# A relational graph layer on one core: 32 counted nodes in place of 16, and another order of the two edge fronts

## The chip, the cores and the metric

The kernel runs on one core of one Trainium2 chip, as a single launch. The metric is device time in microseconds (us). Before the change it is 2970.67 us, the median of three runs (2969.94 to 2975.62). Engines are TensorE (PE; PEld is its weight load), VectorE (DVE), ScalarE (ACT), GpSimd (POOL) and SyncE (SP).

## What is computed

6250 nodes with 256 features, 100000 edges sorted by target node, 8 edge types. Three relational layers, then a small attention, each followed by a residual and a layer norm:

```
for l in range(3):
    xr  = einsum('nd,rde->rne', h, W_rel[l])
    agg = segment_sum(xr[edge_type, src], dst)        # 100000 edges
    h   = relu(agg + h @ W_root[l] + bias[l])
x = layernorm(x + h)
alpha = softmax(leaky_relu(alpha_l[src] + alpha_r[dst]))   # only the first 6250 edges are used
x = layernorm(x + broadcast(sum_h alpha * xt[dst]))
```

The target of an edge is drawn as 6250 u², u uniform, so the lowest nodes have by far the most edges: the first tiles of 128 edges belong to a handful of nodes each.

## The kernel before

**Tiles.** Edges lie in 782 tiles of 128 (one per SBUF partition), nodes in 49 tiles of 128. The kernel does not multiply each edge by a weight. It first sums the *inputs* of the edges by (target, type), and then multiplies the sums by the eight weights.

**One group of the edge loop** (`layer`, the loop `for i in range(NG + 5)`) is up to GT = 4 edge tiles. `gather` (L499) has GpSimd issue one indirect DMA per tile, which fetches 128 source rows of 1 KB into a buffer `msg`. `onehot` (L483, VectorE) makes a 0/1 matrix of the tile's edges against (type, node in window), R·W wide; W, the number of nodes a tile may span, is 3 to 26. `windows` (L516, TensorE) multiplies the rows by it: two matmuls per tile, which the profile shows as two records each, so four records per tile. `add` (L528, VectorE) adds the result, out of PSUM, into a ring of node tiles S, at a place read from `pos`.

**Two fronts.** The edge tiles are walked from two starting points, both downwards: front 0 (the upper, tiles TM = 410 to 781, wide windows, ring of four node tiles) and front 1 (the lower, tiles 36 to 409, narrow windows, ring of three). `Plan.order` mixes the groups of the two: before, one of each in turn, and six groups of the lower front at the end.

**Dense work.** When the last edge tile of a node tile is added, `dense` (L582, L586) multiplies it by W_root and by the eight W_rel: 36 f32 records of 256 columns. It is a generator; every group takes PIECE = 6 steps of it. `finish` (L606, L609 or L613 to L622) adds the bias and stores the tile, `clear` (L595, ScalarE) zeroes its place in the ring. In the third layer `logits` (L636) and `prepare` (L726 to L762) make what the attention needs.

**Hot nodes.** The first HOT = 16 nodes have so many edges that tiles 0 to 35 are left out of the edge loop (TH = 36). For them `count` (L649 to L666), once, in the first layer, counts how often each source row occurs per (node, type): for a pair of node and edge tile VectorE makes a 0/1 matrix `sel` of 392 columns and TensorE adds it up in PSUM; 138 pairs, two per group from group COUNT_AT = 56. `products` (L692), in each layer, multiplies the counts A (f32) with all rows of the node table: 49 matmuls in 13 loads of up to four node tiles, one load and one product in turn per group from group HOT_AT = 130. Its loads are issued by SyncE and take their buffers from the same pool `mp` (eight buffers of four tiles, in turn) as the gathers.

**What orders the work.** Each engine runs its instructions in program order (`manual_schedule`); between engines there are semaphores. Within a group the program has, in this order: steps of `prepare`, `count` and `products`; the gather; `onehot` of the group four ahead; `logits`; `finish` and `clear` of what `dense` ended; the windows; up to six dense steps; the adds; the transposes of the next node tile (`turn`, L560, L563); `fold` (L569, L571). GpSimd may run ahead of TensorE as far as free buffers in `mp` let it.

```
msg = gather(i)
vals = places(i)
...
wins = windows(i, msg, ohs.pop(0))
...
add(i, wins, vals)
```

Of the kernel before, what the change touches and what calls it, by code (L numbers as in the profile page):

```python
# [10 lines left out]
F32 = mybir.dt.float32  # L11
I32 = mybir.dt.int32
BF16 = mybir.dt.bfloat16
AF = mybir.ActivationFunctionType
ALU = mybir.AluOpType
AX = mybir.AxisListType
# [4 lines left out]
P = 128  # L21
EPS = 1e-5
GT = 4
NS = (4, 3)
PAD = 32
MARGIN = 800
HOT = 16
SELS = 6
LOWS = 17
COUNT_AT = 56  # L30
HOT_AT = 130
NEAR = 450
DB = 32
PREP_AT = 164
PIECE = 6
WB = 32
AHEAD = 4
LEAD = 6
GWIN = 256
# [4 lines left out]
class Plan:  # L44
# [35 lines left out]
    def order(self):  # L80

        g = [list(range(k, min(k + GT, self.T))) for k in range(self.TH, self.T, GT)][::-1]
        a = [[t for t in k if t >= self.TM] for k in g if k[-1] >= self.TM]
        b = [[t for t in k if t < self.TM] for k in g if k[0] < self.TM]
        n = max(1, len(b) - LEAD)
        seq, k = [], 0
        for i, g in enumerate(b):
            while k < len(a) and k * n <= i * len(a):
                seq.append((0, a[k]))
                k += 1  # L90
            seq.append((1, g))
        return seq + [(0, g) for g in a[k:]]

# [25 lines left out]
def kernel(  # L119
# [14 lines left out]
    nc = tc.nc  # L134
    N, D = x.shape
    E = src.shape[0]
    L, R = w_rel.shape[0], w_rel.shape[1]
    H, DH = attn_l.shape
    KC = D // P
    pl = Plan(N, E, R)  # L140
    NT, T, CH, WMAX = pl.NT, pl.T, pl.CH, pl.WMAX
# [7 lines left out]
    flag = const.tile([1, 1], I32, name="flag")  # L149
# [3 lines left out]

    bad = nc.values_load(flag[0:1, 0:1], min_val=0, max_val=6 * T)
    with tc.If(bad > 0):
# [3 lines left out]
def fast(tc, const, pl, x, xs, src, dst, edge_type, w_rel, w_root, bias, weight,  # L159
         attn_l, attn_r, out, flag):  # L160
    nc = tc.nc
# [8 lines left out]
    with ExitStack() as top:  # L170
# [16 lines left out]

        A = tab.tile([P, NT, HOT * R], F32, name="A")

# [12 lines left out]
        with ExitStack() as s:  # L202
# [4 lines left out]
            xp = s.enter_context(tc.tile_pool(name="xp", bufs=3))  # L207
            hp = s.enter_context(tc.tile_pool(name="hp", bufs=1))
            ps_w = s.enter_context(tc.tile_pool(name="ps_w", bufs=4, space=PSUM))
# [32 lines left out]
            with tc.manual_schedule():  # L242
                for l in range(L):
                    wr, wo = load_w(l)
                    opn = layer(
                        tc, pl, l, l == L - 1, groups, ready, S, hold, A, hk, hl, idx, key, pos,
                        iota, ident, wr, wo, bias_b, x, xs, eps, w1x, altab, y,
                        (al3, ga, hif, yT0, lane, dst, iota_p),
                        mp, op, xp, hp, ps_w, ps_d, ps_t, H)

# [211 lines left out]

def layer(tc, pl, l, final, groups, ready, S, hold, A, hk, hl, idx, key, pos, iota, ident, wr, wo,
          bias_b, x, xs, eps, w1x, altab, y, att, mp, op, xp, hp, ps_w, ps_d, ps_t, H):
    nc = tc.nc
# [107 lines left out]
    def cols(f, j):  # L573
        at = (j % NS[f]) * P
        return S[f][:, :, at:at + P]
# [64 lines left out]
    def count():  # L640

        lows, made, pc = {}, [], None
        pairs = [(n, t) for n in range(HOT) for t in pl.hot_tiles(n)]
        for m in range(len(pairs) + SELS - 2):
# [13 lines left out]
            if m >= SELS - 2:  # L658
                n, t, oh = made.pop(0)
                tiles = pl.hot_tiles(n)  # L660
                if t == tiles[0]:
                    pc = ps_d.tile([P, 512], F32, name="pd")
                nc.tensor.matmul(pc[:, :NT * R], lows[t], oh, start=(t == tiles[0]),  # L663
                                 stop=(t == tiles[-1]))
                if t == tiles[-1]:
                    nc.scalar.copy(A[:, :, n * R:(n + 1) * R],  # L666
                                   pc[:, :NT * R].rearrange("p (j r) -> p j r", r=R))
            yield

    def products():  # L670
# [14 lines left out]

        sums = hp.tile([P, D], F32, name="sums")
        for js in loads:
            t = load(js)
            yield
            ph = ps_d.tile([P, 512], F32, name="pd")  # L690
            for n, j in enumerate(js):
                nc.tensor.matmul(ph[:, :D], A[:, j], t[:, n], start=(n == 0), stop=(j == js[-1]))  # L692
            yield
            if js[0] == 0:
                nc.vector.tensor_copy(sums, ph[:, :D])
            else:
                nc.vector.tensor_tensor(sums, sums, ph[:, :D], ALU.add)
        pt = ps_t.tile([P, 4 * P], F32, name="pt")
        for k in range(KC):
            nc.tensor.transpose(pt[:, k * P:(k + 1) * P], sums[:, k * P:(k + 1) * P], ident)  # L700
        for k in range(KC):
            o = cols(1, 0)[:, k * R:(k + 1) * R, :HOT]
            nc.vector.tensor_tensor(
                o, o, pt[:, k * P:k * P + HOT * R].rearrange("p (n r) -> p r n", r=R), ALU.add)
        yield
# [79 lines left out]
    for i in range(NG + 5):  # L785
# [4 lines left out]
        for _ in range(2 if i >= COUNT_AT else 0):  # L790
            next(counting, None)
        if i >= HOT_AT:
            next(hot, None)
# [81 lines left out]
def halves(A):  # L875

    v = A.rearrange("p j s -> p (j s)").bitcast(BF16)
    n = v.shape[1] // 2
    return v[:, :n], v[:, n:]
# [498 lines left out]
```

## Time and profile before

| what | value |
|---|---|
| median of the runs shown | 2970.67 us |
| the profiled execution: its time, its span | 2981.72 us, 2980.0 us |
| mean granted TensorE clock | 0.939 |
| busy share: TensorE, its weight loads, VectorE, ScalarE, GpSimd | 90%, 82%, 56%, 15%, 72% |
| gathers by GpSimd (L499) | 2238, of 950 ns each |
| first layer: first gather starts, last ends | 11.3, 946.3 us |
| second layer | 964.8, 1899.3 us |
| third layer | 1919.0, 2867.8 us |
| end of the span | 2980.0 us |
| DMA | 389 MB, mean 131 GB/s |

"Busy" is the time in which an engine had at least one instruction of a group in flight; for TensorE the ends are modelled, so that a group of matmuls has a tail of some 0.2 us in which the next one already runs. The columns of the windows view are: stretch in us, its length, then busy us and number of instructions of each engine, the granted TensorE clock, the share of the DMA engines and GB/s. A line of the waits view says which engine and line waited for which, with the total in us, the number of waits and the longest.

### The profile page before, as it was taken

The page shows a single profiled execution, that of the slowest core. Times are in us where ns is not written, and L with a number is a line of the kernel's source. Part 1 is how long each engine was busy: PE and PEld are TensorE (multiplying, and loading weights), DVE is VectorE, ACT ScalarE, POOL GpSimd, SP SyncE. Part 2 cuts the span into 40 slices and gives each one's busy share as a digit, 9 for nine tenths or more (in the row PEclk, how much of TensorE's full clock was granted, in tenths as well). Part 3 has the DMA queues.
Part 4 walks back from the last instruction along what each step waited for, and adds up shares of the span by engine and source line. Part 5 has one row for each costly group of instructions (what it writes and reads, how often), then busy time and mean ns, then how long its engine had stood idle before and what let it go on. Part 6 is the DMA issues. An engine that isn't in the chain of part 4 may idle for free.

```text
span 2980.0 us, 45437 instructions
## 1 busy us (share of the span) xinstructions
PE 2684.0 (90%) x15806; PEld 2436.3 (82%) x15807; DVE 1664.3 (56%) x4097; ACT 452.7 (15%) x599; POOL 2136.6 (72%) x2254
## 2 busy tenths in 40 slices
PE   5999999999877899998988987789999999999985
PEld 4998888888776788988877887678888888888874
DVE  7555677764432555555454443355556655554768
ACT  2111111111001011111111010111111111110114
POOL 6777777777775777777777777577777777777731
PEclk9999999999988899999999997799999999998985
DMA  4444444445433444444444544344444444454534
GB/s 151 122 124 123 122 120 123 120 133 159 146 116 106 129 123 122 124 124 117 123 117 148 163 126 117 118 123 127 130 124 128 124 125 128 136 176 137 167 114 167
DMA packets 203054, 388.99 MB, mean 131 GB/s; under 512 B 42885, under 2 KB 128004, under 8 KB 202820
## 3 DMA queue, kind: packets, MB, share of 16 engines
q0 software_dynamic: 107424, 293.48, 34.2%
q1 hardware_dynamic: 92200, 89.76, 9.4%
q8 instruction: 131, 2.15, 0.3%
q10 hardware_dynamic: 3196, 2.76, 0.3%
q14 instruction: 103, 0.84, 0.1%
HBM read 360.18 MB, written 25.65 MB: 129 GB/s over the span
## 4 chain that ended last, share of the span: by engine, by line
PE 70%; POOL 10%; issue 8%; DVE 6%; DMA 3%; ACT 2%; DVEq 0%; ACTq 0%; POOLq 0%; SPq 0%
PE pw L516 31%; PE pd L586 31%; POOL msg L499 10%; PE pd L582 4%; DMA msg<-x,idx 2%; DVE S L528 2%; PE pd L692 1%; PE pt L560 1%; PE pt L636 1%; ACT xT L563 1%; DMA msg<-in_x_dram,idx 1%; PE pd L663 1%; DVE st L1034 0%; DVE z L1022 0%; PE pw L749 0%
## 5 line engine op out<-in xcount | busy, mean ns | idle before, releaser
L499 POOL DMA_INDIRECT msg<-x,idx x1492 | 1417.2, 950 | 504.3 <-issue 420.2
L516 PE MATMUL pw<-oh,msg 128*128 128x160 f32 (+22 forms) x8952 | 1300.7, 302 | 187.4 <-DMA msg<-x,idx 95.2
L528 DVE TENSOR_TENSOR S<-S,pw 128x320 f32 (+22 forms) x2238 | 904.3, 404 | 989.5 <-PE pd L586 504.3
L516 PEld LDWEIGHTS pw<-oh,msg 128*128 128x128 f32 x8952 | 1245.0, 201 | 253.6 <-issue 109.6
L586 PE MATMUL pd<-wr,S 128*128 128x256 f32 x4800 | 1130.9, 386 | 2.2 <-DVE S L528 1.9
L586 PEld LDWEIGHTS pd<-wr,S 128*128 128x128 f32 x4800 | 913.2, 194 | 122.6 <-DVE S L528 3.9
L499 POOL DMA_INDIRECT msg<-in_x_dram,idx x746 | 708.0, 949 | 236.4 <-issue 209.7
L483 DVE TENSOR_TENSOR oh<-iota,key 128x640 f32<-128x640 f32 (+23 forms) x564 | 363.9, 647 | 25.6 <-issue 13.9
L595 ACT ACTIVATE S<-S 128x2048 uint32<-128x2048 uint32 x150 | 285.0, 1900 | 25.9 <-PE pd L586 25.9
L563 ACT COPY xT<-pt 128x256 f32<-128x256 f32 x195 | 72.4, 371 | 1048.1 <-PE pt L560 1046.7
L609 ACT ACTIVATE h<-pd 128x256 f32<-128x256 f32 x98 | 37.7, 385 | 903.3 <-DVE pd L606 669.0
L582 PE MATMUL pd<-wo,xT 128*128 128x256 f32 x588 | 167.8, 411 | 3.2 <-ACT h L609 3.2
L606 DVE TENSOR_TENSOR pd<-pd,bias_b 128x256 f32<-128x256 f32 x147 | 63.2, 430 | 186.6 <-PE pd L586 186.4
L582 PEld LDWEIGHTS pd<-wo,xT 128*128 128x128 f32 x588 | 109.3, 203 | 12.9 <-ACT h L609 3.6
L654 DVE TENSOR_SCALAR sel<-iota,hk 128x392 bf16<-128x392 f32 x138 | 80.4, 613 | 0.0
L619 ACT ACTIVATE rs<-mv,eps 128x1 f32<-128x1 f32 x49 | 14.4, 295 | 403.8 <-DVE mv L618 403.8
L692 PE MATMUL pd<-msg,A 128*128 128x256 f32 x294 | 71.9, 387 | 1.9 <-DMA msg<-x 1.9
L692 PEld LDWEIGHTS pd<-msg,A 128*128 128x128 f32 x294 | 55.6, 196 | 9.1 <-issue 2.2
L560 PE MATMUL pt<-ident,xin 128*128 128x128 f32 x294 | 58.3, 281 | 1.4 <-ACT xT L563 1.4
L636 PEld LDWEIGHTS pt<-w1x,xT 128*128 128x128 f32 x192 | 26.6, 201 | 35.3 <-ACT xT L563 35.3
L560 PEld LDWEIGHTS pt<-ident,xin 128*128 128x128 f32 x294 | 41.8, 147 | 13.2 <-ACT xT L563 2.8
L636 PE MATMUL pt<-w1x,xT 128*128 128x4 f32 x192 | 30.8, 266 | 23.6 <-ACT xT L563 23.6
(187 smaller groups left out, 629.3 us busy)
## 6 DMA issues: line engine op xcount, KB each, us to landing
msg<-x,idx POOLq DMA_INDIRECT x1492, 2.8
x<-h SPq DMA_DIRECT2D x96, 128.0 KB
xin<-x SPq DMA_DIRECT2D x96, 128.0 KB
msg<-x SPq DMA_DIRECT2D x24, 512.0 KB
msg<-in_x_dram,idx POOLq DMA_INDIRECT x746, 2.8
y<-yt SPq DMA_DIRECT2D x49, 128.0 KB
xin<-in_x_dram SPq DMA_DIRECT2D x48, 128.0 KB
msg<-in_x_dram SPq DMA_DIRECT2D x12, 512.0 KB
```

Source lines behind the costliest of these rows:

```text
L483: nc.vector.tensor_tensor(oh[:, :len(g), :w], iota[:, :w].unsqueeze(1).to_broadcast([P, len(g), w]), key[:, g[0]:g[-1] + 1].unsqueeze(2).t ...
L499: nc.gpsimd.indirect_dma_start(out=msg[:, q, :], out_offset=None, in_=table, in_offset=bass.IndirectOffsetOnAxis(ap=idx[:, t:t + 1], axis=0))
L516: nc.tensor.matmul(pw[:, k * w:(k + 1) * w], msg[:, q, k * P:(k + 1) * P], oh[:, q, :w], start=True, stop=True)
L528: ins = nc.vector.tensor_tensor(o, o, pw.rearrange("p (a b) -> p a b", b=W), ALU.add)
L560: nc.tensor.transpose(pt[:, k * P:(k + 1) * P], t[:, k * P:(k + 1) * P], ident)
L563: nc.scalar.copy(xT.rearrange("p k n -> p (k n)"), pt[:, :D])
L582: nc.tensor.matmul(pd[:, :D], xT[:, k], wo[:, k], start=(k == 0), stop=False)
L586: i = nc.tensor.matmul(pd[:, :D], s[:, k * R + r], wr[:, k, r], start=(xT is None and k == r == 0), stop=(k == KC - 1 and r == R - 1))
L595: i = nc.scalar.memzero(cols(f, j))
L636: nc.tensor.matmul(pt[:, :H], yT[:, k], w1x[:, k, D + H:D + 2 * H], start=(k == 0), stop=(k == KC - 1))
L654: nc.vector.tensor_scalar(oh, iota[:, :NT * R], float(512 * n), hk[:, t:t + 1], op0=ALU.add, op1=ALU.is_equal)
L692: nc.tensor.matmul(ph[:, :D], A[:, j], t[:, n], start=(n == 0), stop=(j == js[-1]))
```

## The change

Two things are changed, with the constants that place them.

**More counted nodes.** HOT goes from 16 to 32. Tiles 0 to 51 are now left out of the edge loop (TH = 52; 730 tiles stay in each layer, in 184 groups instead of 188). `count` has 272 pairs instead of 138, starts at group 8, and in addition takes the largest count of each node; a few small operations at its end raise the flag that selects the general path if a count passes 256. A is now bf16, twice as wide (256 columns per node tile, the same bytes). `products` therefore works in bf16: each load of rows is split into three bf16 parts that add up to the f32 value (`x3`: a ScalarE copy, a VectorE subtraction in place, a ScalarE copy in one group; a second VectorE subtraction in the next), and for each node tile there are 2 halves × 3 parts = 6 matmuls of 256 columns. The next load is issued before the current one is split. It starts at group 148 in the first layer and at group 118 in the other two.

**Another order.** The lower front gets more than its share of the groups at first, the upper one at the end (SLOW = 0.3); the last six groups are of the lower front as before. PREP_AT moves from 164 to 149.

```diff
-HOT = 16
+HOT = 32
-COUNT_AT = 56
-HOT_AT = 130
+COUNT_AT = 8
+HOT_AT = 148, 118
-PREP_AT = 164
+PREP_AT = 149
+SLOW = 0.3
...
         n = max(1, len(b) - LEAD)
         seq, k = [], 0
-        for i, g in enumerate(b):
-            while k < len(a) and k * n <= i * len(a):
+        for i in range(len(a) + n):
+            u = (i + 1) / (len(a) + n)
+            want = len(a) * (u - SLOW * u * (1 - u))
+            if k < len(a) and (k + 0.5 <= want or i - k >= n):
                 seq.append((0, a[k]))
                 k += 1
-            seq.append((1, g))
-        return seq + [(0, g) for g in a[k:]]
+            else:
+                seq.append((1, b[i - k]))
+        return seq + [(1, g) for g in b[n:]]
...
-        A = tab.tile([P, NT, HOT * R], F32, name="A")
+        A = tab.tile([P, NT, HOT * R], BF16, name="A")
...
                     nc.scalar.copy(A[:, :, n * R:(n + 1) * R],
                                    pc[:, :NT * R].rearrange("p (j r) -> p j r", r=R))
+                    nc.vector.tensor_reduce(top[:, n:n + 1], pc[:, :NT * R], AX.X, ALU.max)
...
-        sums = hp.tile([P, D], F32, name="sums")
-        for js in loads:
-            t = load(js)
+        HH = HOT * R // P
+        HN = HOT // HH
+        sums = hp.tile([P, HH * D], F32, name="sums")
+        x3 = hp.tile([P, 3, GT * D], BF16, name="x3")
+        rows_of, ph, m = {0: load(loads[0])}, None, 0
+        yield
+        for m, js in enumerate(loads):
+            if m + 1 < len(loads):
+                rows_of[m + 1] = load(loads[m + 1])
+            w = len(js) * D
+            t = rows_of.pop(m).rearrange("p a d -> p (a d)")[:, :w]
+            nc.scalar.copy(x3[:, 0, :w], t)
+            nc.vector.tensor_tensor(t, t, x3[:, 0, :w], ALU.subtract)
+            nc.scalar.copy(x3[:, 1, :w], t)
             yield
+            nc.vector.tensor_tensor(x3[:, 2, :w], t, x3[:, 1, :w], ALU.subtract)
             ph = ps_d.tile([P, 512], F32, name="pd")
-            for n, j in enumerate(js):
-                nc.tensor.matmul(ph[:, :D], A[:, j], t[:, n], start=(n == 0), stop=(j == js[-1]))
+            for h in range(HH):
+                for n, j in enumerate(js):
+                    for c in range(3):
+                        nc.tensor.matmul(ph[:, h * D:(h + 1) * D], A[:, j, h * P:(h + 1) * P],
+                                         x3[:, c, n * D:(n + 1) * D], start=(n == c == 0),
+                                         stop=(j == js[-1] and c == 2))
             yield
-            if js[0] == 0:
-                nc.vector.tensor_copy(sums, ph[:, :D])
+            if m == 0:
+                nc.vector.tensor_copy(sums, ph[:, :HH * D])
             else:
-                nc.vector.tensor_tensor(sums, sums, ph[:, :D], ALU.add)
+                nc.vector.tensor_tensor(sums, sums, ph[:, :HH * D], ALU.add)
...
-        if i >= HOT_AT:
+        if i >= HOT_AT[min(l, 1)]:
             next(hot, None)
```

The pool `hp`, which holds the small tiles of `count` and `products`, is now opened anew for each layer.

## The prediction

> **What bounds the kernel now.** I read the page's groups first, then the windows, the waits and the timeline. The page names TensorE (90%), but its busy time has modelled ends. The groups of the gathers:
>
> ```profile
> L499 POOL DMA_INDIRECT msg<-x,idx x1492 | 1417.2, 950 | 504.3 <-issue 420.2
> L499 POOL DMA_INDIRECT msg<-in_x_dram,idx x746 | 708.0, 949 | 236.4 <-issue 209.7
> ```
>
> Nearly all of GpSimd's idle time is "issue": 0.30 us after each gather, in which it waits for nothing. From the first gather of the second layer (964.8) to the last (1899.3) are 934.5 us for 746 gathers, 1.2527 us each, 5.01 us a group of four. That pace hardly changes anywhere (last bracket but the clock: GpSimd):
>
> ```profile
> 1200.00:1250.00 50.00, 49.18 (x291) 45.27 (x290) 28.05 (x58) 7.67 (x9) 37.81 (x41) 1.00 0.43 122
> 1850.00:1900.00 50.00, 41.26 (x219) 37.43 (x219) 14.84 (x51) 5.11 (x6) 37.42 (x40) 0.76 0.39 113
> 2300.00:2350.00 50.00, 47.35 (x290) 42.59 (x289) 30.78 (x74) 7.69 (x12) 37.33 (x39) 1.00 0.44 126
> ```
>
> So GpSimd paces layers one and two, with TensorE close behind. The waits of TensorE alone, second layer and third:
>
> ```profile
> PE pw L516 <- DMA msg<-x,idx: 73.5, 35, 10.8
> ...
> PE pw L516 <- DVE S L528: 13.6, 26, 0.9
> ```
>
> ```profile
> PE pw L516 <- DMA msg<-x,idx: 21.7, 8, 10.2
> ```
>
> In the second layer TensorE waits 73.5 us for gathers: slack. In the third it waits 21.7 us, all in the first 55 us of that layer. From then on it runs behind: the timeline has the gathers of group 60 issued by 2220.2 and its windows at 2258.2, 38 us later, close to the eight buffers' limit. The third layer is TensorE's.
>
> **What it does in a group.** TensorE in the second layer:
>
> ```profile
> 1177.16 1.93 PE L516 MATMUL pw<-oh,msg 128*128 128x104 f32 x16
> 1178.93 1.05 PE L582 MATMUL pd<-wo,xT 128*128 128x256 f32 x4
> 1179.81 1.89 PE L586 MATMUL pd<-wr,S 128*128 128x256 f32 x8
> 1181.54 0.38 PE L560 MATMUL pt<-ident,xin 128*128 128x128 f32 x2
> 1181.76 2.66 PE L516 MATMUL pw<-oh,msg 128*128 128x184 f32 x16
> 1184.25 2.75 PE L586 MATMUL pd<-wr,S 128*128 128x256 f32 x12
> ```
>
> From start to start: 111 ns a window record of 104 columns (1178.93 − 1177.16, over 16), 156 ns at 184, 216 ns a dense record. VectorE, third layer, one group:
>
> ```profile
> 2209.59 2.75 PE L586 MATMUL pd<-wr,S 128*128 128x256 f32 x12
> ...
> 2212.38 2.32 DVE L528 TENSOR_TENSOR S<-S,pw 128x368 f32 x4 [5.03 <-PE pd L586]
> ...
> 2212.97 2.02 PE L516 MATMUL pw<-oh,msg 128*128 128x96 f32 x16 [0.41 <-DVE S L528]
> ```
>
> The adds of a group can wait for the dense records that still read their ring, and then end (2214.7) after TensorE has moved on (2212.97). This decides below.
>
> **The skill.** Perfetto Trace Analysis, GPSIMD Engine Instruction, says to time GpSimd by the spacing of its instructions: done above, 1.25 us against a span of 0.95. TensorE: Matmul & The Clock Gate, "Wait — 56ns, not 53.3ns?", gives N/2.4 + 2.5 ns from start to start when warm: the trace agrees, 84 ns for the bf16 records of 196 columns (L749), 166 for 392 (L663), and 216 for an f32 record of 256, which is 512 by the formula. VectorE: DVE Perf Modes, Mode 1×, has one f32 result a cycle, 1.04 ns; here `onehot` takes 1008 ns for 832 elements and 578 for 416, 1.03 ns each.
>
> **The change, part by part.**
>
> *Fewer gathers.* 16 tiles a layer less: GpSimd 16 × 1.2527 = 20.0 us a layer, 60 in all. TensorE 16 × 4 records × 0.111 (spacing) to 0.119 (busy time of the narrow ones) = 7.1 to 7.6 us a layer, of which only the third layer's counts.
>
> *Products.* TensorE had 98 f32 records × 0.216 = 21.2 us a layer and gets 49 × 6 = 294 bf16 ones of 256 columns. The trace has none of that size; the formula gives 0.109, half an f32 record 0.108; L749's busy time per record, scaled to 256, 0.134. I take 0.109: 32.1 us, so +10.9 (to +18). With the windows, +3.3 us a layer. Each of the 13 steps, one in two groups, adds on VectorE two operations of 1024 elements (1.0 + 0.19 us by the rows above, some 1.2 us each) and on ScalarE two copies of about 1.03 us (371 ns at 256, 1900 at 2048). SyncE issues as many loads as before.
>
> *The wait that comes with them.* The second subtraction stands on VectorE behind the adds of the group before, and TensorE's 24 product records, with that group's windows behind them, wait for it. From the timeline I took, for groups 20 to 59 of each layer, when VectorE was through with a group and when TensorE began the next windows: 1.25 us of extra work in between would have kept TensorE waiting 1.2 us in the mean in all three layers, and 1.65 and 1.35 in groups 60 to 124 of the first and third. Bounds: 0, if VectorE uses the slower pace to get ahead; 3.4 in the group shown. I take 1.4: 18.2 us a layer.
>
> *The buffers.* A load now holds its buffer until that subtraction, three groups after it was issued, instead of until the product of the next group. Counting eight buffers on in the order of allocation, every second gather waits for the subtraction two groups before it; before, none waited for less than four groups back. GpSimd can then lead by two groups, and TensorE's lag behind it, 4.3 us at the least (landing and windows), can only grow to about 10 us. So in this stretch of 29 groups GpSimd is held to TensorE's pace, past 5.5 us of grace, and what it loses there it doesn't make up.
>
> *The stretch, second layer (groups 118 to 146).* 464 window records 56.7, 132 dense matmuls 57.0, transposes 1.5, products 32.1: 147.3 us, times 1.045 (the saturated stretches of the first layer, 20 to 120, took 4 to 6% over such sums) 153.9, and 18.2 of waits: 172.1. GpSimd alone would take 29 × 5.01 = 145.3. Loss 26.8 − 5.5 = 21.3. The layer: −20.0 + 21.3 = **+1**. Outside the stretch the sums are 3.6 to 4.8 us a group, under 5.01.
>
> *First layer (148 to 176).* 135.8 × 1.045 + 18.2 = 160.1, loss 14.8 − 5.5 = 9.3. Counting gets 134 more pairs: TensorE 134 × 0.166 = 22 us (0.253 by busy time: 34), VectorE 134 × 0.613 + 32 maxima × 0.5 + 16 × 0.34 = 104 us, ScalarE 16 × 0.49. Spread over groups 8 to 145 it raises VectorE from 27 to about 42 of 50 us; TensorE's sum stays under GpSimd's (groups 10 to 147: about 675 with 5%, against 691). I put 5 us on later adds (0 to 30) and 3 on the lag left at the end, since only seven groups follow. −20.0 + 9.3 + 8 = **−3**.
>
> *Third layer.* TensorE's: fewer gathers give nothing. +3.3, +18.2, and +4 since the new order puts less of its work (27 us, not 31) under the first ten groups, where it waits for gathers. Late in the layer its groups 140 to 180 took 39 us over their sums where 18 is usual, at a granted clock of 0.83 to 1.0; with upper groups there and `prepare` spread over 35 groups I give back 8 of these 21 (0 to 20). **+17**.
>
> *The order by itself.* In the second layer its sums per 20 groups go from 4.0, 5.2, 4.8, 4.5, 4.2, 4.1, 4.2, 3.9, 3.3 us a group to 3.8, 4.7, 4.7, 4.5, 4.3, 4.0, 5.4, 4.1, 3.5: smoother, but the early peak was buffered. It gains nothing where GpSimd paces. Reopening a pool per layer: nothing, its tiles are long free.
>
> Sum: −3 + 1 + 17 = +15, against the profiled span of 2980.0 (1.7 us lie outside); I lay it on the median, 2970.7 + 15 = 2986.
>
> **Rivals.** The measurement can tell about 0.2%, 6 us, from no change.
> - *The wait is hidden, faster.* If products wait only 0.3 us, 14 us a layer go: the second −13, the first −12 (its loss ends at 0), the third +3, and 3 to 5 more if its end warms up: about −25, 2945. For it: VectorE is idle 44% of the time. Against: the row of 5.03 us above, 105 such waits. The turning point is 1.0 us a step; above it the change loses.
> - *Counting makes the first layer TensorE's.* At 84% VectorE recovers half as fast from each late add; 4% on 820 us is 33: 3014. For it: TensorE waits for adds already. Against: counting at 72% (350 to 650) cost no more than the groups before it.
> - *They cancel* within 6 us, at a wait of about 1.0: 2971.
>
> **How the numbers follow.** Forecast (2977 to 3008) 0.49, second rival 0.12, first 0.27, third 0.12. Faster 0.27, same 0.12, slower 0.61. The range 2936 to 3018 leaves out the first rival's lower end (all 20 us in two layers) and the second's upper one, about 0.1.
>
> **What would show it.** 2190 gathers at 1.25 us; in the stretches GpSimd waiting for VectorE's subtraction or falling under 41 gathers in 50 us, and TensorE waiting at the products for `x3`, 1.4 us a time. The third layer no shorter than 949 us from first to last gather. Wrong if the products start without a wait, if the first two layers both shrink by over 12 us, or if the third shrinks.

## The result and the profile after

The changed kernel takes 3093.9 us, median of four runs (3092.36 to 3094.86), against 2971.5 us for the kernel before beside it: ratio 1.0409, 95% interval 1.0391 to 1.0427. It is 4.1% slower. The forecast was 2986, up to 3018; the sign was right and the size was not.

The profiled execution has a span of 3092.2 us at a mean clock of 0.940; before it was 2980.0 at 0.939. The page's groups of the gathers, and the new one of the products (count | busy us, mean ns | idle before it, and what ended most of that):

```profile
L505 POOL DMA_INDIRECT msg<-x,idx x1460 | 1405.5, 963 | 563.3 <-issue 411.8
L726 PE MATMUL pd<-x,A 128*128 128x256 bf16 x882 | 132.8, 311 | 73.5 <-DVE x L721 54.4
```

The work went as the change says: 2190 gathers, not 2238. But a gather has become longer in the mean (963 ns for 950), and GpSimd's idle time ahead of the gathers of the second and third layer has grown from 504.3 to 563.3 us although there are 32 fewer; "issue" accounts for less of it than before (411.8 of it, not 420.2), so the growth is waiting. The windows view, one line from the stretch of each layer in which products run:

```profile
900.00:950.00 50.00, 39.58 (x279) 34.76 (x278) 28.78 (x56) 12.67 (x14) 35.50 (x33) 0.97 0.42 125
1650.00:1700.00 50.00, 41.99 (x276) 37.23 (x275) 25.50 (x49) 11.93 (x14) 34.95 (x33) 0.93 0.47 143
2590.00:2640.00 50.00, 42.20 (x257) 38.64 (x258) 29.08 (x60) 10.38 (x13) 26.97 (x26) 0.90 0.42 127
```

The last bracket before the clock is GpSimd's: 33, 33 and 26 instructions in 50 us, where the kernel before had 39 to 41. TensorE, which by the forecast was to hold it up, is busy for only 40 to 42 of the 50 us: it waits too. For what, the waits view of the whole kernel says (total us, number, longest):

```profile
ACT x L719 <- DVE msg L718: 159.5, 39, 9.1
POOL msg L505 <- PE pw L522: 146.7, 126, 11.0
...
PE pd L726 <- DVE x L721: 54.4, 26, 4.0
...
PE pt L642 <- ACT xT L569: 36.0, 48, 5.1
...
PE pd L670 <- DVE top L675: 20.0, 9, 3.0
PE pd L726 <- ACT x L719: 19.1, 10, 2.3
```

GpSimd's wait for a buffer that windows still read is 146.7 us; before the change it was 43.3:

```profile
POOL msg L499 <- PE pw L516: 43.3, 108, 3.5
```

For the subtraction itself (L721), which the prediction had named as what a gather would wait for, GpSimd waits only 1.8 us in the whole kernel. TensorE waits at the products for both engines of the split, 54.4 and 19.1 us, and in the first layer at the counts (L670) for the new maximum (L675).

From the timeline of the gathers and of each group's windows I worked out where the 112.2 us of longer span lie. (The medians differ by 122.4 us. The profiled execution of the kernel before, at 2981.7 us, was itself 10 us over its median, so these 10 us are not in the table.) "Stretch" is the 29 groups beside the products, and "lag" is the time from the end of a group's last gather to its first window record.

| piece | before, us | after, us | difference | forecast |
|---|---|---|---|---|
| start to first gather | 11.3 | 12.4 | +1.1 | |
| first layer, groups 0 to 147 | 737.5 | 757.5 | +20.0 | +8 |
| its stretch, 148 to 176 | 145.2 | 195.2 | +50.0 | +9.3 |
| its rest | 52.3 | 31.4 | −20.9 | −20 |
| between first and second layer | 18.5 | 30.2 | +11.7 | |
| second layer, groups 0 to 117 | 586.9 | 587.8 | +0.9 | |
| its stretch, 118 to 146 | 145.2 | 172.6 | +27.4 | +21.3 |
| its rest | 202.4 | 181.4 | −21.0 | −20 |
| between second and third layer | 19.7 | 18.5 | −1.2 | |
| third layer, groups 0 to 117 | 594.8 | 589.2 | −5.6 | |
| its stretch, 118 to 146 | 150.6 | 206.6 | +56.0 | |
| its rest | 203.3 | 182.6 | −20.7 | |
| third layer in all | 948.7 | 978.4 | +29.7 | +17 |
| last gather to the end | 112.2 | 126.8 | +14.6 | |

The four groups less give their 20 us in every layer, the third too, for which the prediction had put nothing. They are spent in the stretch, more than twice over in the first and third layer.

One step of the second layer's stretch in the timeline (start, duration, engine and line; in brackets the idle time before it and what ended it):

```profile
1668.14 1.22 DVE L718 TENSOR_TENSOR msg<-msg,x 128x1024 f32<-128x1024 f32 x1
1668.19 1.99 POOL L505 DMA_INDIRECT msg<-x,idx  x1 [0.30 <-issue]
...
1669.39 1.04 ACT L719 CAST x<-msg 128x1024 bf16<-128x1024 f32 x1 [1.40 <-DVE msg L718]
1669.98 2.19 DVE L534 TENSOR_TENSOR S<-S,pw 128x304 f32 x4
...
1672.99 2.46 POOL L505 DMA_INDIRECT msg<-x,idx  x1 [0.30 <-issue]
1673.06 0.48 DVE L577 MEMSET S<- 128x512 f32 x1 [0.17 <-DVE S L575]
1673.47 1.16 DVE L721 TENSOR_TENSOR x<-msg,x 128x1024 bf16<-128x1024 f32 x1
...
1674.68 4.54 PE L726 MATMUL pd<-x,A 128*128 128x256 bf16 x22 [3.92 <-DVE x L721]
...
1679.06 1.89 PE L522 MATMUL pw<-oh,msg 128*128 128x56 f32 x16
```

The second subtraction (L721) comes behind the adds and the fold of the group before; TensorE stands still for 3.92 us. Then 22 of its product records take 4.54 us, 206 ns each; elsewhere in this stretch, when they start without a wait, 24 take 2.62 us, 109 ns each. The windows view over these microseconds shows why:

```profile
1670.00:1674.60 4.60, 0.27 (x1) 0.10 (x1) 4.08 (x9) 0.44 (x1) 3.69 (x4) 0.71 0.42 125
1674.60:1677.00 2.40, 2.32 (x12) 1.59 (x12) 0.72 (x2) 0.00 (x0) 1.79 (x3) 0.50 0.18 55
1677.00:1679.00 2.00, 2.00 (x12) 1.45 (x11) 0.00 (x0) 0.00 (x0) 1.70 (x2) 0.56 0.42 109
1679.00:1682.00 3.00, 3.00 (x24) 2.87 (x23) 0.92 (x4) 1.04 (x1) 2.09 (x3) 1.00 0.36 107
```

The granted clock after the wait is 0.50 for some 4 us, then 1.00. A long wait at the products is paid twice. The Trainium skill, TensorE: Matmul & The Clock Gate, section "What's actually happening", states it: an idle window of about 3.4 us brings TensorE to half its clock, and about as long a busy one brings it back. This trace agrees in kind, but less was enough here. In the three stretches TensorE waits over 0.5 us at 26 of the 39 steps; the 14 steps whose waits add up to 2.9 us or more were each followed by half clock, of 3.4 or 6.8 us, and the 12 of 1.9 us or less by none.

In several sets of runs everything, the kernel before included, took a fifth longer (3594 to 3626 us for the kernel before), for a reason that stays open; the nine results that fell there stand at the end of the experiments, and nothing is built on them.

### The profile page after: what moved, and what is told of

The parts are those of the page before. It is cut to its first block, busy times and chain, and to the rows that moved or that the text cites. A ratio compares the mean times of both kernels' runs of the same rounds, so it can differ in the third digit from the quotient of the medians.

```text
span 3092.2 us, 47013 instructions
## 1 busy us (share of the span) xinstructions
PE 2723.2 (88%) x16344; PEld 2443.3 (79%) x16345; DVE 1835.5 (59%) x4365; ACT 540.2 (17%) x701; POOL 2122.2 (69%) x2214
## 4 chain that ended last, share of the span: by engine, by line
PE 48%; POOL 8%; DVE 7%; issue 6%; DMA 3%; ACT 2%; DVEq 0%; ACTq 0%; POOLq 0%
PE pd L592 19%; PE pw L522 19%; POOL msg L505 8%; PE pd L726 3%; DMA msg<-x,idx 3%; DVE S L534 3%; PE pd L588 2%; PE pt L642 1%; DVE x L721 1%; PE pt L566 1%; PE p L1056 1%; ACT xT L569 1%; DVE oh L489 0%; DVE s L1024 0%; DVE msg L718 0%
## 5 line engine op out<-in xcount | busy, mean ns | idle before, releaser
L505 POOL DMA_INDIRECT msg<-x,idx x1460 | 1405.5, 963 | 563.3 <-issue 411.8
L534 DVE TENSOR_TENSOR S<-S,pw 128x240 f32 (+21 forms) x2190 | 893.5, 408 | 963.2 <-PE pd L592 524.3
L522 PE MATMUL pw<-oh,msg 128*128 128x80 f32 (+22 forms) x8760 | 1259.9, 300 | 140.8 <-DMA msg<-x,idx 81.1
L522 PEld LDWEIGHTS pw<-oh,msg 128*128 128x128 f32 x8760 | 1202.6, 199 | 227.2 <-issue 111.2
L726 PE MATMUL pd<-x,A 128*128 128x256 bf16 x882 | 132.8, 311 | 73.5 <-DVE x L721 54.4
L726 PEld LDWEIGHTS <-A 128*128 128x128 bf16 x882 | 97.8, 111 | 103.0 <-issue 79.9
L661 DVE TENSOR_SCALAR sel<-iota,hk 128x392 bf16<-128x392 f32 x272 | 158.7, 614 | 0.0
L588 PEld LDWEIGHTS pd<-wo,xT 128*128 128x128 f32 x588 | 106.7, 199 | 19.2 <-ACT h L615 10.5
L670 PE MATMUL pd<-sel,low 128*128 128x392 bf16 x272 | 69.3, 330 | 21.7 <-DVE top L675 20.0
L719 ACT CAST x<-msg 128x1024 bf16<-128x1024 f32 (+1 forms) x39 | 38.8, 996 | 159.5 <-DVE msg L718 159.5
```

The source lines that it names most:

```text
L505: nc.gpsimd.indirect_dma_start(out=msg[:, q, :], out_offset=None, in_=table, in_offset=bass.IndirectOffsetOnAxis(ap=idx[:, t:t + 1], axis=0))
L522: nc.tensor.matmul(pw[:, k * w:(k + 1) * w], msg[:, q, k * P:(k + 1) * P], oh[:, q, :w], start=True, stop=True)
L534: ins = nc.vector.tensor_tensor(o, o, pw.rearrange("p (a b) -> p a b", b=W), ALU.add)
L588: nc.tensor.matmul(pd[:, :D], xT[:, k], wo[:, k], start=(k == 0), stop=False)
L661: nc.vector.tensor_scalar(oh, iota[:, :NT * R], float(512 * n), hk[:, t:t + 1], op0=ALU.add, op1=ALU.is_equal)
L726: nc.tensor.matmul(ph[:, h * D:(h + 1) * D], A[:, j, h * P:(h + 1) * P], x3[:, c, n * D:(n + 1) * D], start=(n == c == 0), stop=(j == js[- ...
```

## The experiments

The theory after the result: the split into three parts is the main cost, by the wait at the products, the half clock after it, and GpSimd's short lead. The maxima on VectorE are the second. The rivals: the new order, the mere number of products, and the buffers that each load keeps.

**Which half of the change?** The kernel before with the new `order` and SLOW = 0.3 alone (HOT 16, PREP_AT 164):

> The kernel before with the new order of the fronts alone (16 counted nodes, f32 products, all placements as before). Theory 1, the split chain of the products: the order costs nothing where GpSimd paces; the attention works in 10 parts instead of 9 because 7 instead of 6 tiles are open when prepare begins, +2 us; the third layer up to 6 us shorter: 2964 to 2978 us. Rival, the order is what costs: over 3010 us.

Measured: 2979.2 us, ratio 1.0025 [1.0014, 1.0035], span 2978.3; 1 us over my range. Its layers are 933.5, 934.2 and 942.5 us; the third is 6 us shorter than before, and from the last gather to the end it takes 117.8 us and not 112.2. The other half, the changed kernel with the old `order`:

> The changed kernel with the order of the fronts as before. Theory 1: nearly all of the +122 us stays, less some 6 for the attention (13 parts instead of 17): 3070 to 3100 us, with GpSimd held in the three stretches of products by 130 us or more in all. Rival, the order is what costs: under 3010 us.

Measured: 3115.1 us, 1.0478 [1.0457, 1.0498], 15 us over my range; layers 974.8, 943.8 and 1002.6. So the counts bring the whole loss. The order by itself costs 0.25%, 9 us, which the two profiles can't place, since that of the kernel before was 10 us over its median. Beside the counts it takes 21 us off: 24 in the third layer and 12 after the last gather, against 9 more in the first. It is no cause of the 112 us, but perhaps for a part at the tail.

**Is it the split?** One bf16 part of each row; the second and third are left out, and with them both subtractions, a ScalarE copy and two thirds of the product matmuls:

```diff
-            nc.vector.tensor_tensor(t, t, x3[:, 0, :w], ALU.subtract)
-            nc.scalar.copy(x3[:, 1, :w], t)
             yield
-            nc.vector.tensor_tensor(x3[:, 2, :w], t, x3[:, 1, :w], ALU.subtract)
...
-                    for c in range(3):
+                    for c in range(1):
...
```

> The changed kernel with one bf16 part of the rows instead of three: the second and third part (two VectorE subtractions, one ScalarE copy and two thirds of the product matmuls) are left out, so the sums of the counted nodes are only as exact as bf16. Theory 1: TensorE no longer waits for VectorE at the products and the row buffers come free one group earlier; the three stretches fall from 195, 172 and 207 us of GpSimd to about 150, 147 and 155: 2980 to 3005 us, and no gather longer than 1.2 us. Rival, the matmuls and the counting cost and not the chain: only the 21 us of matmuls in each of the TensorE-bound layers go, 3040 to 3060 us.

Measured: 2954.7 us, 0.9941 [0.9921, 0.9961]: 139 us less than the changed kernel, more than I expected. The layers are 947.2, 914.0 and 919.5 us. The second is 20.5 us under its 934.5 before the change: the whole of the gathers' gain, with nothing paid. Its page has the gathers at their old length:

```profile
L505 POOL DMA_INDIRECT msg<-x,idx x1460 | 1386.0, 949 | 484.9 <-issue 401.5
```

**The chain or the number of products?** Two parts; the third is left out. VectorE's first subtraction writes the second part, and L719 and L721 go; 16 products a step and not 24:

```diff
-            nc.vector.tensor_tensor(t, t, x3[:, 0, :w], ALU.subtract)
-            nc.scalar.copy(x3[:, 1, :w], t)
+            nc.vector.tensor_tensor(x3[:, 1, :w], t, x3[:, 0, :w], ALU.subtract)
             yield
-            nc.vector.tensor_tensor(x3[:, 2, :w], t, x3[:, 1, :w], ALU.subtract)
...
-                    for c in range(3):
+                    for c in range(2):
...
```

> The kernel of two_parts once more, for the same reason: the third part of each row left out, so that ScalarE's second copy, VectorE's second subtraction and a third of the product matmuls go, and the products are of about 16 bits instead of 24. Theory 1 (the chain of four dependent steps over two engines): the waits at the products fall to under 6 us a layer, and the whole is 2965 to 2985. Rival (the price goes with the number of products on TensorE): about half of the 139 us between one part and three, 3020 to 3030.

Measured: 2981.3 us, 1.0020 [1.0013, 1.0027]. The second part costs 27 us over one part, the third 113. The number of products, 98 a part and layer, is the same for both steps; what the third part adds alone is a second copy and a subtraction behind it in the same step, and with them the later release of the rows' buffer. The price doesn't go with the products. Nor is it that they only now reach GpSimd's pace: TensorE's own time for the second layer's stretch grows by 5 us with the second part and by 38 with the third (table below).

**TensorE's wait or GpSimd's buffers?** Both changed in the second layer only, so that the other two layers serve as a control. First, the same instructions, with the parts in two buffers in turn and the products of a step issued one step later, so that they find their parts ready; the rows still go through GpSimd's ring:

```diff
+                x3 = hp.tile([P, 3, GT * D], BF16, name="x3", bufs=2)
+                ph = multiply(*prev[1:]) if prev else None
             nc.scalar.copy(x3[:, 0, :w], t)
...
             nc.vector.tensor_tensor(x3[:, 2, :w], t, x3[:, 1, :w], ALU.subtract)
+                prev = m, js, x3
```

> The kernel of split_ahead_l2 once more (that run, with three others, was on a chip on which the kernel before took 3594 us instead of 2970, so that it can't be set beside the changed kernel's 3094). Second layer alone: parts in two buffers in turn, products one step later. Theory 1: the 26 us of waits at the products of that layer and most of the 10 us of slower records go, TensorE's stretch falls from 187 to 152 to 165, and the layer from 941.8 to 920 to 930, the whole to 3074 to 3084. Rival (the buffer that each step keeps for itself stops GpSimd): the waits go, but GpSimd's stretch stays above 168, and the whole at 3088 or more.

Measured: 3079.9 us, 1.0357 [1.0326, 1.0389]; the layer 926.2. Second, nothing moved on any engine, but two buffers of their own for the rows:

```diff
-            t = mp.tile([P, GT, D], F32, name="msg")
+            t = (hp.tile([P, GT, D], F32, name="rows", bufs=2) if l == 1
+                 else mp.tile([P, GT, D], F32, name="msg"))
```

> As for own_rows_l2[...]: the product rows of the second layer in two buffers of their own. Theory 1 (TensorE's waits for the split): TensorE's stretch stays at 185 to 190 us and the layer within 4 us of 941.8. Rival (the ring buffer kept by each step): GpSimd's 17 us of gaps in that stretch go to under 5, and the layer to 925 to 930.

Measured: 3079.5 us, 1.0362 [1.0332, 1.0392]; the layer 927.1. My theory had this one at no change, and it fell: it was the rival's number. The stretch of the second layer in five kernels, from their timelines (us; "TensorE" and "GpSimd" are the time that each takes for it; gaps are GpSimd's idle time beyond 0.31 us a gather; "longer" is the gathers' time over 0.96 us each):

| kernel | TensorE | GpSimd | gaps | longer | layer |
|---|---|---|---|---|---|
| after | 187.4 | 172.5 | 17.3 | 9.8 | 941.8 |
| own_rows_l2_again | 186.9 | 154.1 | 0.0 | 8.9 | 927.1 |
| split_ahead_l2_again | 158.5 | 157.8 | 0.0 | 12.5 | 926.2 |
| two_parts_again | 149.5 | 150.8 | 0.0 | 5.3 | 921.2 |
| one_part | 144.5 | 145.3 | 0.0 | 0.3 | 914.0 |

With two more buffers TensorE is as slow as ever, and it no longer matters. The waits in the stretch, the changed kernel first, then the one with the rows apart:

```profile
PE pd L726 <- DVE x L721: 18.4, 9, 3.9
POOL msg L505 <- PE pw L522: 18.4, 8, 4.6
```

```profile
PE pd L727 <- DVE x L722: 15.8, 7, 4.3
...
POOL msg L505 <- PE pw L522: 0.3, 1, 0.3
```

TensorE's wait for the split stays, GpSimd's wait for a buffer is gone. TensorE's lag grows to 34 us at group 147 (19 in the changed kernel) and is 3.4 us again at group 176: the layer's later groups are light enough to work off the arrears, if GpSimd is allowed to run on. So in this layer the gaps take both, a slow TensorE and a short lead; removing either removes them. For the first and third layer no run took the two apart. What is left over the one-part kernel's 914.0 is mostly the longer gathers.

**The maxima.** The changed kernel without the 32 maximum reductions (L675) and the flag operations at their end, which are left out:

```diff
-                    nc.vector.tensor_reduce(top[:, n:n + 1], pc[:, :NT * R], AX.X, ALU.max)
```

> The changed kernel without the largest count of each node (32 reductions and the few operations that raise the flag are left out, so counts over 256 go unnoticed). Theory 2, the reductions make VectorE wait for ScalarE and TensorE for VectorE (20.0 us of waits at the count matmuls): the first layer 20 to 35 us shorter, 3060 to 3074 us. Rival, the 134 more 0/1 matrices make VectorE late and the reductions only show it: within 10 us of the changed kernel, 3084 to 3100 us.

Measured: 3058.3 us, 1.0293 [1.0276, 1.0311], 35.6 us less, slightly more than I expected. The first layer is 946.6 and not 984.1 us. Waits of the first layer between 313 and 790 us, some 90 groups ahead of the stretch, the changed kernel, then without the maxima:

```profile
POOL msg L505 <- PE pw L522: 24.3, 31, 3.6
...
PE pd L670 <- DVE top L675: 18.4, 8, 3.0
```

```profile
POOL msg L505 <- PE pw L522: 8.6, 20, 1.4
```

The maximum reads the PSUM bank which the next node's count needs, and on VectorE it stands behind the adds: TensorE waits up to 3.0 us for an operation of 0.56 us. Before it can begin, VectorE itself waits for ScalarE's copy of the same counts (L673), 13.9 us in 12 waits over the layer. GpSimd's buffers fill behind it. By group 148 TensorE's lag is 28 us, and without the maxima 5. The 37.5 us saved divide into 12.5 before the stretch and 25 in it. The 25 look like a lead given back: with the products' loads in the ring GpSimd can't keep the 28 us by which it is ahead. The kernel with one part points the same way. It starts the stretch with the same 28 us, its TensorE isn't late there (134.0 us), and still GpSimd has 14.5 us of gaps; best_third below, which starts with 5, has none. No run gave the loads their own buffers in this layer.

**The tail.** The changed kernel with PREP_AT = 164:

> The changed kernel with the preparation of the attention from group 164. The theory has changed: in the kernel with all three undoings the last steps of the preparation come after the last window, 10 us on the chain that ends last, because in the new order few groups of the lower front are left after group 164, and the preparation advances only with those. So the parts' 17 instead of 9 and the late steps nearly cancel: from last window to end 101 to 104 us as against the changed kernel's 104.2, and the whole at 3090 to 3094. The first theory (the parts alone): 92 to 95 us there, and 3080 to 3083.

Measured: 3087.7 us, 1.0390 [1.0359, 1.0420]; from last gather to end 123.3 us, not 126.8, and from last window to end 105.1, not 104.2. My first theory, that the attention's 17 parts (9 before) alone make the tail longer, is refuted; the second said 3090 to 3094 and was 2 us off. In the chain that ended last, the preparation's last steps now lie behind the last window, at 2998 to 3005 us:

```profile
2998.45 0.48 DVE picks L798
2998.95 0.86 DVE ga L802
2999.84 0.58 DVE picks L798
3000.44 0.85 DVE ga L802
```

From last window to end the kernel before takes 92.3 us (old order, group 164); order_only 101.7 (new order, 164), with the same steps in its chain; counts_only 102.1 (old order, 149, 13 parts); the changed kernel 104.2 (new order, 149, 17 parts). `prepare` advances only in groups of the lower front, and the new order has 12 of these after group 164 where the old has 15 (order_only; the changed kernel has 11). So it seems that one either begins it sooner, has more tiles open and so more and smaller parts, or pays for its last steps at the end: about 10 us either way, and not twice. That the two nearly cancel is read from these five figures; no run removed both.

**All three undone.** Two parts (the third left out), the maximum taken once from the finished counts in SBUF, and PREP_AT = 164; the 32 counted nodes and the new order stay:

```diff
-                    nc.vector.tensor_reduce(top[:, n:n + 1], pc[:, :NT * R], AX.X, ALU.max)
+        for j in range(0, NT, 2):
+            b = min(j + 2, NT)
+            nc.vector.tensor_reduce(top[:, j:b], A[:, j:b, :], AX.X, ALU.max)
+            yield
```

> As for best_again: two bf16 parts instead of three, the maximum taken once from the finished counts in SBUF, preparation from group 164. If the three costs are separate: 2930 to 2945, below both kernels, and a tail of 110 to 114 us. Rival (the same stall counted twice): 2955 to 2970.

Measured: 2946.6 us, 0.9926 [0.9900, 0.9951]: below both kernels, a little over my range; its tail of 116.8 us is over it too. The three single effects add up to 112.6 + 35.6 + 6.2 = 154.4, which makes 2939.5; it is 7 us above that, so they are nearly separate. Its layers are 926.1, 919.9 and 930.8 us, all shorter than before, and its page reads

```profile
L505 POOL DMA_INDIRECT msg<-x,idx x1460 | 1394.4, 955 | 495.2 <-issue 398.1
```

with the gathers' idle time under the 504.3 us of before, and their length half way between.

**The nine results set aside.** These are the kernels of own_rows_l2_again, split_ahead_l2_again, prep164_fifth, two_parts_again and best_third, beside a kernel before of 3594 us in the first four, 3626 in the next two, 3597 in the two after, and 3602 in the last. Their absolute forecasts can't be held against such times. In own_rows_l2 TensorE's lag is 37 us in the median over all groups (19 in own_rows_l2_again), so TensorE and not GpSimd sets the pace nearly everywhere, and the prices above need not hold.

> The changed kernel, but in the second layer alone the rows for the products are loaded into two buffers of their own and no longer into GpSimd's ring of eight; the chain of the split and its order on every engine stay. Theory 1 (TensorE's waits for the split, which GpSimd then follows through the buffers that TensorE empties late): TensorE's stretch stays at 185 to 190 us, and the layer stays within 4 us of its 941.8 from first to last gather, so the whole stays at 3090 to 3095. Rival (the ring buffer that each step keeps for itself is what stops GpSimd): GpSimd's 17 us of gaps in that stretch go to under 5, and the whole goes to 3076 to 3082.

Measured: 3666.5 us, ratio 1.0205 [1.0165, 1.0244].

> The changed kernel, but in the second layer alone the three parts lie in two buffers in turn and the products of a step are issued one step later, behind the next group's copies, so that TensorE finds its parts ready; the same instructions otherwise, and the rows still go through GpSimd's ring. Theory 1: the 30 us of waits at the products of that layer and the 10 us of slower records after them go, TensorE's stretch falls from 187 to about 152 to 160, the gathers' lengthening of 10 us stays, GpSimd's stretch falls from 172.5 to 155 to 160, and the whole to 3076 to 3083. Rival (the ring): the waits go but GpSimd's stretch stays above 168, and the whole at 3088 or more.

Measured: 3671.4 us, 1.0219 [1.0178, 1.0260].

> The changed kernel with the preparation of the attention begun from group 164, as before, and not from 149, so that by the trace's counting 6 tiles instead of 10 are still open then and the attention comes in 9 parts instead of 17. Theory (the tail of the changed kernel is 14.6 us longer because of those parts): the tail from last gather to end falls from 126.8 to 112 to 115 and the whole to 3080 to 3083. Rival (the tail is longer because TensorE is behind at the last gather): no less than 3090.

Measured: 3687.1 us, 1.0267 [1.0226, 1.0308].

> The changed kernel with two bf16 parts of each row instead of three: ScalarE's second copy, VectorE's second subtraction and a third of the product matmuls are left out; VectorE's one subtraction writes the second part and leaves the loaded row as it is. The products are thereby of about 16 bits instead of 24. Theory 1 (the chain of four dependent steps over two engines): one subtraction ahead of the step is short enough to be ready, the waits at the products fall to under 6 us a layer, half of the gathers' lengthening stays (4 to 5 us a layer), and the whole is 2965 to 2985. Rival (the price goes with the number of products on TensorE): half of the 139 us between one part and three, 3020 to 3030.

Measured: 3652.5 us, 1.0162 [1.0122, 1.0202].

> The changed kernel with the preparation of the attention begun from group 164, as before, and not from 149, so that by the trace's counting 6 tiles instead of 10 are still open then and the attention comes in 9 parts instead of 17.[...] Theory (the tail of the changed kernel is 14.6 us longer because of those parts): the tail from last gather to end falls from 126.8 to 112 to 115, and the whole to 3080 to 3083. Rival (the tail is longer because TensorE is behind at the last gather): no less than 3090.

Measured: 3711.2 us, 1.0229 [1.0182, 1.0276].

> Three undoings together: two bf16 parts instead of three (the third left out, so that the products are of about 16 bits), the maximum taken from the finished counts in SBUF, two node tiles at a time, and not from PSUM at each count, with a threshold one lower, and the preparation from group 164. The rest of the change stays: counts for 32 nodes, the new order. If the three costs are separate, as Theory says: 2981 less 33 for the maxima and less 12 for the tail, 2930 to 2945, below both kernels. Rival (the time that the maxima and the split cost is the same stall counted twice, in the transition and the full buffers): 2955 to 2970.

Measured: 3653.6 us, 1.0055 [1.0023, 1.0088].

> As for prep164_again[...]: preparation of the attention from group 164, 6 open tiles instead of 10, 9 parts of attention instead of 17. Theory: the tail from last gather to end falls from 126.8 to 112 to 115 and the whole to 3080 to 3083. Rival (TensorE's arrears at the last gather): no less than 3090.

Measured: 3688.7 us, 1.0238 [1.0183, 1.0292].

> As for best[...]: two bf16 parts instead of three (the third left out: products of about 16 bits), the maximum taken once from the finished counts in SBUF, preparation from group 164. If the three costs are separate: 2930 to 2945, below both kernels. Rival (the same stall counted twice): 2955 to 2970.

Measured: 3619.3 us, 1.0066 [1.0044, 1.0088].

> The changed kernel with the preparation of the attention from group 164, 6 open tiles instead of 10, 9 parts of attention instead of 17. Theory (the parts make the tail longer): the tail from last gather to end falls from 126.8 to 112 to 118, and the whole to 3080 to 3086. Rival (TensorE's arrears at the last gather make it): no less than 3090.

Measured: 3696.0 us, 1.0246 [1.0213, 1.0279]. What follows from the nine together: even the kernel with all three undoings isn't faster than before there, so its 0.7% is not a gain under all conditions.

## Why the prediction was right in sign and wrong in size

- **The gain of fewer gathers** was right for two layers: 20.0 us a layer foretold, 20.5 in the one-part kernel's second layer, and nearly 21 in the rest of each layer. For the third I wrote "fewer gathers give nothing", and that was wrong: its rest is 20.7 us shorter as well, and the one-part kernel's third layer is 29.2 us shorter than before, of which the order alone gives 6.2.
- **The products** were right: 109 ns a record, 24 in 2.62 us, where they start without a wait. TensorE's warm sums held as well: 147.3 us foretold for the second stretch, 147.7 from the records there.
- **"I take 1.4"** for the wait was too little. In the second stretch the waits at the products are 18.4 us for VectorE and 5.5 for ScalarE's copy (L719), which I had not counted: 1.8 us in each of 13 steps, and 2.1 in the first layer (18.7 and 8.1). The half clock adds less than it seems: slower records make some 9 us of TensorE's 187.4, but they made nearly 8 in the same groups before, after waits for gathers, and the factor 1.045 had 6.6 for them. I had 172.1 for TensorE there, and 160.1 in the first layer, where it took 180.4.
- **"In this stretch … past 5.5 us of grace, and what it loses there it doesn't make up"** is, beside that wait, the step that failed most. I had counted that a gather waits for the subtraction two groups before it and that the lag can only grow to about 10 us. Neither is in the trace: GpSimd waits for windows, and in the second layer TensorE's lag went from 4 to 19, a grace of nearer 15 us, so that a TensorE 42 us slower than GpSimd's pace cost 17.3 us of gaps and 9.8 of longer gathers. Why the count of the buffers fell short stays open. It is luck that too small a wait and too small a grace nearly offset each other there: +7.3 for a forecast of +1. In the first layer the grace was below nothing: TensorE was already 28 us behind at group 148, and 16 at group 176, so GpSimd lost TensorE's slowness, 35 us, and 12 us of its own lead. I had 9.3 us; it was 50.0, the largest miss, of which TensorE's slowness beyond my 160.1 is 20 us and the lead most of the rest.
- **Counting**, "5 us on later adds", was 20.0 us before the stretch. Of these 12.5 are the maxima; the 7.5 that stay without them are near my figure. I priced the 32 maxima by their 0.5 us and not by who waits for the bank that they read. The rival "counting makes the first layer TensorE's", at 0.12, had 33 us; the maxima are worth 35.6. That the two are close is luck: the late step was the maximum, not the adds.
- **Between the first and second layer** I had no term, and it was 11.7 us. It belongs to the split: without the maxima this piece is 30.2 us as well, with one part 19.2. TensorE is still 16 us behind at group 176, and only seven groups follow.
- **The third layer** was +29.7 and not +17, and even that hides two errors: the stretch cost 56.0 us, and the layer's other groups, where I had put no gain, took 26 of them back. The split's waits in its stretch are 17.4 us for VectorE and 5.5 for ScalarE, and a wait that I hadn't named is beside them: the logits' for the turned row, 16.4 us. Before, in the same groups, it was 4.0. The two views, before and after:

```profile
PE pt L636 <- ACT xT L563: 4.0, 8, 0.5
```

```profile
POOL msg L505 <- PE pw L522: 40.3, 8, 11.0
...
PE pt L642 <- ACT xT L569: 16.4, 8, 5.1
```

The 8 waits have become four times as long in sum, and the longest 5.1 us where it was 0.5: on ScalarE the row's copy comes behind the split's copies, which themselves wait for VectorE (L719, 159.5 us). I costed ScalarE's two copies by their 1.03 us and not by what queues behind their wait. No run moved the copies alone, but the third part is what brings this wait: in the same groups it is 3.6 us with the new order alone, 3.8 with one part and 3.3 with two, where L719 is left out.

- **The order "gains nothing"**: nearly right for the order alone (1.0025), and it cost some 9 us after the last window (101.7 for 92.3), 5.6 of them seen from the last gather, that my sum left out. Moving PREP_AT I had priced only by what it takes off the third layer's end.
- **Longer gathers** had no place in the sum: 8 to 10 us a stretch, shown below.

Forecast and result are 108 us apart, and 97 of these show in the two profiles (112.2 less 15). Of the 97, 52 are the first layer's, 10.5 the transitions', 6 the second layer's, 13 the third's, 15 the tail's and 1 the start's.

## What to carry to other kernels

Price a step that crosses engines by its place in each queue, not by its operations: here the third part, with a copy, a 1.2 us subtraction and 98 products a layer, cost 113 us, and 32 maxima of 0.56 us on a half-idle VectorE cost 36, since TensorE stood behind them. A leading engine's loss is the slower engine's arrears beyond what the buffers let it run ahead, so ask at each stage how much lag has already been used up; two buffers or a step of distance between making and using can be worth as much as removing the work. And when an order is changed, look up which generators advance only in some of its groups.

## What the runs showed of the hardware that I had not expected

A gather's instruction on GpSimd grows when VectorE runs an operation with two SBUF inputs. In the changed kernel 105 gathers overlap one of the 78 subtractions (L718, L721), and 50 of them take over 1.1 us; each of the 50 ends 813 to 829 ns after the subtraction's end. With one subtraction a step (two_parts_again) it is 27 of 61, with the same 813 to 822 ns. With none (one_part) 18 gathers in all take over 1.1 us, and 13 of these end 814 to 822 ns after the addition in `fold`, which has two SBUF inputs too; in the kernel before it is 10 of 15. In the timeline above the two gathers of 1.99 and 2.46 us are of this kind. In the second layer's stretch the lengthening is 9.8, 5.3 and 0.3 us for two, one and no subtractions. The Trainium skill names it (GPSIMD Engine Reference, "8. Key points": contention with VectorE instructions that have two SBUF inputs); the adds and `onehot`, with one input in PSUM, show nothing like it here.

What decides is a moment early in the gather. In the changed kernel, of 49 gathers with a subtraction running from no later than 0.13 us after their start to at least 0.30 us after it, 46 took over 1.1 us; of 42 in which a subtraction began later than 0.13 us, 2 did. Of 571 gathers with an add or a `onehot` running over that moment, and no two-SBUF operation, none did. The subtractions are not held up in turn: those that begin during a gather take 1218 ns in the median, the others 1217.
